# Two expert layers on TensorE: second layer as seven block products (Strassen) instead of eight, in 128x64 tiles

## The chip, the cores and the metric

The kernel runs on one core of a Trainium2 chip. A core has five engines with an instruction queue each: PE (TensorE, matrix products), DVE (VectorE), ACT (ScalarE), POOL (GpSimd) and SP (SyncE, which issues most transfers here). They work on SBUF, a memory of 128 partitions, and on PSUM, eight banks of 128 partitions x 512 f32 in which PE leaves and adds up its products. An instruction waits at the head of its queue for the semaphores that it names, and what stands behind it waits too.

The metric is the device time of one launch, in microseconds (us). All data are f32.

## The reference

The input x is 16 batches of 256 tokens with 128 channels. Four steps each add to x what they compute from its layer norm: attention a (binarized weights, 16 heads of 8), a feed-forward layer of experts, attention b (16 heads, relative positions), and the same expert layer again with the same weights. The expert layer is:

```python
logits = einsum('bld,ed->ble', x, gate_weight)          # 8 experts
kth_val = sort(logits.reshape(-1))[expert_k - 1]         # one threshold over all tokens and experts
gates = logits * (logits >= kth_val)
h = gelu(einsum('bld,ehd->bleh', x, w1) + b1)            # 512 hidden units an expert, tanh form
y = einsum('bleh,edh->blde', h, w2) + b2.T[None, None]
out = einsum('blde,ble->bld', y, gates)
```

All eight experts are computed for every token, and a gate that fails the threshold is a zero factor.

## The kernel before

The kernel is one program for the four steps. An expert layer works on chunks of 512 tokens (`CH`), eight of them, channels on the partitions. One expert on one chunk is called a unit here: 64 units a layer, 128 in all. A unit has a hidden half and an output half, both in `experts`' helpers:

- `h_unit` (L1104, L1106), four times: one matmul of 128 hidden units x 512 tokens, and a gelu on ScalarE that moves the bank to SBUF. Four times 128 hidden units make the expert's 512.
- `y_unit` (L1115): four matmuls that add up, over the 512 hidden units, the 128 output channels x 512 tokens in one bank.
- `gated` (L1231 to L1235): VectorE adds the expert's bias b2 to the bank, multiplies by the gates (`gb`: one gate per token, the same on all partitions) and adds the result to the chunk's accumulator `acc` in SBUF. `gb` comes from `broadcast_gates` (L1209), a transfer that SyncE issues, 256 KB written for 2 KB of gates.
- `residual` (L1258, L1261): when a chunk's eight experts are in `acc`, PE transposes it to token order and VectorE adds it to x.

An f32 matmul is two PE instructions (two passes over the moving data). While PE does the hidden half of unit i, the output half of unit i-1 follows it, so gelu has the time of an output half.

Gates are known only after the threshold, and that comes from a search (`search`, L1157 to L1203: counts on VectorE, small matmuls, 20 rounds) that starts when all logits of the layer are there. So the first `EARLY` = 16 units of each layer are computed without gates: their outputs with bias wait as `raw` tiles (L1134) in SBUF. These early units are interleaved with the end of the attention before (L886, L901, L920 for attention b) and with the search. When the gates exist (L1276, L1282 to L1285), they are multiplied and added (`gated` with bias None), one per late unit, while the other 48 units run.

Between the two layers, attention b begins inside the first: `begin` gives pieces of its preparation (L692 to L832) that are called at four of the last twelve units, and the last chunk's sum of layer one is added to x by `add_late` (L1059, L1064) when attention b is already running.

The order on PE during the search is written by hand; elsewhere a scheduler orders each engine's queue by the program's order, dependences and free buffers.

## Time and profile before

| what | value |
|---|---|
| time, median of 3 runs (lowest, highest) | 1531.12 us (1530.74, 1531.26) |
| span of the profiled execution | 1528.8 us, at full granted clock |
| time outside the span, median less span | 2.3 us |
| PE busy | 1518.9 us, 99% |
| ACT busy | 838.8 us, 55% |
| VectorE busy | 799.5 us, 52% |
| GpSimd busy | 406.0 us, 27% |
| hidden-half matmuls, 1024 instructions | 461.3 us |
| output-half matmuls, 1032 instructions | 462.4 us |
| first early output gated, layer one and two | 400.3 us, 1250.2 us from the span's start |

The time of the profiled execution itself is its span plus what lies around it; the 2.3 us is the difference to the median of the timed runs. Busy times of pipelined matmuls overlap a little, so a line's mean duration (593 ns) is longer than the distance between two starts. In the 40 slices of the page, GpSimd shows 0 or 1 in all slices of the late units and 8 in attention b; VectorE shows 1 to 4 in late units, ScalarE 3 to 5.

A row of a group reads: line, engine, operation, output <- inputs, partitions x elements, number of instructions, then busy microseconds and mean nanoseconds of one, then the engine's idle time just ahead of them and what ended it.

### The profile page before, as it was taken

To read this page: it belongs to the slowest core of one execution; us is meant where nothing else is said; L and a number is where in the kernel's file an instruction comes from. 1 tells how busy PE (TensorE), PEld (TensorE's weight loads), DVE (VectorE), ACT (ScalarE), POOL (GpSimd) and SP (SyncE) were. 2 spreads that over 40 slices of the span, in tenths; PEclk is the share of its full clock that TensorE was granted. 3 is DMA by queue.
4 is the path that set the end of the run, shared out by engine and by line. 5 is a ranking of instruction groups with operands and counts; after the bars stand their busy time and mean duration, and the time that the engine had idled before them with its cause. 6 is when DMAs were issued, how large, how long until landed. Compare 5 with 4: busy or idle time off the path is not lost. (4 is left out here: it accounts for less than half of the span.)

```text
span 1528.8 us, 30857 instructions
## 1 busy us (share of the span) xinstructions
PE 1518.9 (99%) x12284; PEld 856.0 (56%) x12284; DVE 799.5 (52%) x1622; ACT 838.8 (55%) x2092; POOL 406.0 (27%) x521
## 2 busy tenths in 40 slices
PE   9999999999999999999999999999999999999998
PEld 6777777544444444444677777777444444444444
DVE  7878887334334221212799999999244233222212
ACT  4666666645434343443688888888554443434342
POOL 6333321200001000002488898886100000000000
PEclk9999999999999999999999999999999999999999
DMA  4511110000223211121122222221000432111110
GB/s 108 150 30 32 40 30 16 2 7 1 74 74 79 53 37 39 37 46 28 29 54 56 55 51 46 53 56 37 8 1 2 105 87 79 53 44 40 43 41 8
DMA packets 174128, 69.91 MB, mean 46 GB/s; under 512 B 74521, under 2 KB 173601, under 8 KB 173729
## 3 DMA queue, kind: packets, MB, share of 16 engines
q1 hardware_dynamic: 173408, 67.54, 18.9%
q8 instruction: 97, 1.59, 0.4%
q10 hardware_dynamic: 576, 0.41, 0.1%
q14 instruction: 47, 0.38, 0.1%
HBM read 50.88 MB, written 12.58 MB: 42 GB/s over the span
## 5 line engine op out<-in xcount | busy, mean ns | idle before, releaser
L1106 ACT ACTIVATE hT<-ph,head 128x512 f32<-128x512 f32 x512 | 351.2, 687 | 415.3 <-PE ph L1104 412.5
L1115 PE MATMUL py<-hT,w 128*128 128x512 f32 (+1 forms) x1032 | 462.4, 591 | 1.0 <-ACT logits L987 0.5
L1104 PE MATMUL ph<-xn,w 128*128 128x512 f32 x1024 | 461.3, 593 | 1.1 <-ACT hT L1106 1.1
L1104 PEld LDWEIGHTS ph<-xn,w 128*128 128x128 f32 x1024 | 192.7, 190 | 237.0 <-issue 232.4
L1115 PEld LDWEIGHTS py<-hT,w 128*128 128x128 f32 x1032 | 193.7, 190 | 229.7 <-issue 223.4
L1233 DVE SCALAR_TENSOR_TENSOR gy<-py,head,gb 128x512 f32<-128x512 f32 x83 | 62.3, 751 | 427.5 <-PE py L1115 427.5
L901 ACT ACTIVATE b_pr<-b_s,b_nm 128x256 f32<-128x256 f32 x512 | 235.5, 472 | 59.2 <-DVE b_nm L896 59.0
L455 DVE TENSOR_REDUCE a_nm<-a_s 128x2 f32<-128x512 f32 x256 | 158.6, 683 | 50.3 <-PE a_t L478 48.7
L896 DVE TENSOR_REDUCE b_nm<-b_s 128x4 f32<-128x1024 f32 x128 | 152.7, 1193 | 20.1 <-PE b_s L886 19.9
L886 PE MATMUL b_s<-b_kT,b_qd 64*64 64x256 f32 x1024 | 159.8, 382 | 0.0
L911 DVE STREAM_TRANSPOSE b_pT<-b_pr 128x1024 f32<-128x1024 f32 x128 | 157.1, 1228 | 0.0
L886 PE MATMUL b_s<-strip,b_qb 64*64 64x256 f32 x2048 | 156.6, 376 | 0.0
L886 PE MATMUL b_s<-b_kS,b_qd 64*64 64x256 f32 x1024 | 156.5, 382 | 0.0
L484 ACT ACTIVATE a_pT<-a_t 128x512 f32<-128x512 f32 x256 | 132.5, 603 | 29.2 <-PE a_t L478 28.9
L478 PE MATMUL a_t<-a_qa,a_qk 32*128 32x256 f32 x1024 | 133.8, 392 | 0.1
L776 POOL TENSOR_TENSOR b_qd<-b_qsel,head 128x512 f32<-128x512 f32 x64 | 84.1, 1335 | 177.2 <-DMA b_qsel<-b_qT 168.0
L450 PE MATMUL a_s<-a_qk 32*128 32x256 f32 x1024 | 128.2, 389 | 0.3 <-ACT a_qkc L416 0.3
L153 POOL TENSOR_SCALAR ve<-mv 128x2 f32<-128x2 f32 x64 | 14.7, 230 | 418.8 <-DVE mv L150 408.8
L901 ACT ACTIVATION_READ_ACCUMULATOR b_pr<-b_s,b_nm 128x1 f32 x512 | 104.1, 203 | 0.0
L450 PEld LDWEIGHTS a_s<-a_qk 32*128 32x128 f32 x1024 | 91.5, 184 | 22.6 <-issue 14.9
L478 PEld LDWEIGHTS a_t<-a_qa,a_qk 32*128 32x128 f32 x1024 | 99.6, 184 | 4.0 <-PE a_t L478 0.8
L162 POOL TENSOR_SCALAR xn<-x,mv,rstd 128x128 f32<-128x128 f32 x126 | 99.7, 800 | 6.6
(180 smaller groups left out, 1428.4 us busy)
## 6 DMA issues: line engine op xcount, KB each, us to landing
gb<-gd SPq DMA_DIRECT2D x128, 256.0 KB
w<-in_w SPq DMA_DIRECT2D x2, 2048.0 KB
a_qks<-a_qkc SPq DMA_DIRECT2D x15, 256.0 KB
a_qk<-a_qks SPq DMA_DIRECT2D x60, 64.0 KB
x<-in_x SPq DMA_DIRECT2D x16, 128.0 KB
b_qs<-b_qT SPq DMA_DIRECT2D x64, 32.0 KB
b_qsel<-b_qT SPq DMA_DIRECT2D x64, 32.0 KB
b_z<-b_qs SPq DMA_DIRECT2D x16, 128.0 KB
```

The costliest lines, as they stand in the source:

```text
L162: (last or nc.gpsimd).tensor_scalar(xn[:, t, :], xs[b][:, t, :], mv[:, t, 0:1], rstd[:, t : t + 1], ALU.subtract, ALU.mult,)
L450: nc.tensor.matmul(sc[:, t, :], q[b][rows, g, t * P : (t + 1) * P], k[b][rows, g, :], start=True, stop=True,)
L455: nc.vector.tensor_reduce(nms[G % 4][:, :, j, 0:1].rearrange("p t o -> p (t o)"), sc, AX.X, ALU.max, negate=True,)
L478: nc.tensor.matmul(sc[:, t, :], k[b][rows, g, t * P : (t + 1) * P], qaug[G][rows, :], start=True, stop=True,)
L484: nc.scalar.activation(pT, sc, AF.Exp)
L886: nc.tensor.matmul(sc[64 * c : 64 * c + 64, r, u, :], (qb_[rows, at, c] if rel else qd[rows, at, x]).rearrange("p h q -> p (h q)"), strip[ ...
L896: nc.vector.tensor_reduce(nm, sc, AX.X, ALU.max, negate=True)
L901: nc.scalar.activation(pr[:, u, r, :], sc[:, r, u, :], AF.Exp, bias=nm[:, r, u : u + 1], scale=1.0, accum_out=sums[b][:, n : n + 1],)
L911: nc.vector.transpose(pT[:, half % 2, 4 * i : 4 * i + 4].rearrange("p n k h q -> p (n k h q)"), probs.pop(U).rearrange("p u r k -> p (u r ...
L1104: nc.tensor.matmul(ph, w1[:, m * P : (m + 1) * P], xn2[c], start=True, stop=True)
L1106: nc.scalar.activation(hT, ph, AF.Gelu_apprx_tanh, bias=b1[:, m : m + 1], scale=1.0)
L1115: nc.tensor.matmul(py[:, 0:width], w2[:, e * NHC + k, :], hs[k], start=k == 0, stop=k == NHC - 1)
```

## The change

The output half of the late units is written as a Strassen product (in Winograd's form). The 512 hidden units and 512 tokens of `y = w2 h` are cut in blocks: two halves of the output channels (64 each), two halves of the hidden units (256 each), two halves of the tokens (256 each). The ordinary product takes eight block products of 64 channels x 256 hidden units x 256 tokens; the new form takes seven, on sums and differences of the blocks.

- `hidden`: a matmul of 128 hidden units is split into two of 64, on the left and right half of PE's columns (128x64 tiles). The gelu of 128x512 is as before.
- `mix_hidden`, on VectorE: both halves of the hidden values are multiplied by the gates (2 instructions of 128x1024), and four differences of 128x512 are made. On GpSimd: bias times gates, and its sum over a chunk's experts.
- `mix_weights`, on GpSimd, once per expert and layer: four sums and differences of weights, 128x128 each, kept in the buffers of the raw tiles.
- `products`, on PE: 14 matmuls of 256 tokens (7 products, two halves of the contraction each), in pairs on the two column halves. All experts of a chunk add up in two PSUM banks, so there is no accumulation on VectorE.
- `combine`, once per chunk: ScalarE copies the two banks, SyncE issues three transfers that swap partition halves, GpSimd adds the parts and the bias sum.
- `EARLY` is 18. Four early outputs are gated in the first late slot, then one in each slot; the adds of the latter go to GpSimd.
- The last chunk of the second layer keeps the old form (`plain`). The order of the late units is written by hand for all five engines; gates are fetched a slot ahead, behind the transfers of `combine`; residuals come at slots 15, 28 and the end (41 in the second layer); `begin` has three pieces instead of four, at slots 15, 28 and 34; `add_late` comes one round later; the bias copy `bv` is made at the start of attention b.

```diff
@@ -28 @@
-EARLY = 2 * NE
+EARLY = 2 * NE + 2
...
@@ -702 @@
 
         bo = wpool.tile([P, C], F32, tag="bo", name="b_bo_")
 
+        bv = wpool.tile([P, P], F32, tag="bv", name="b_bv_")
+        nc.vector.tensor_copy(bv, b_bv.to_broadcast([P, P]))
+
         def output_bias(pt):
-            bv = wpool.tile([P, P], F32, tag="bv", name="b_bv_")
-            nc.vector.tensor_copy(bv, b_bv.to_broadcast([P, P]))
             nc.tensor.matmul(pt, bv, wb["o"], start=True, stop=True)
             nc.vector.tensor_tensor(bo, b_bo, pt, ALU.add)
 
...
-                if U == 2:
+                if U == NU + 2:
                     add_late()
                 if U < total:
                     scores(U)
@@ -1141 @@
     def experts(last, place, raw, filling, middle, late):
 
         with ExitStack() as st:
-            hpool = st.enter_context(tc.tile_pool(name="f_h", bufs=1))
             pool = st.enter_context(tc.tile_pool(name="f_2", bufs=2))
-            psum = st.enter_context(tc.tile_pool(name="f_ps", bufs=1, space=PSUM))
+            at_first = st.enter_context(ExitStack())
+            hpool = at_first.enter_context(tc.tile_pool(name="f_h", bufs=1))
+            psum = at_first.enter_context(tc.tile_pool(name="f_ps", bufs=1, space=PSUM))
...
             def broadcast_gates(c, e):
-                gb = pool.tile([P, CH], F32, tag="gb", name=f"gb{c}_{e}", bufs=7 if last else 6)
+                gb = pool.tile([P, CH], F32, tag="gb", name=f"gb{c}_{e}", bufs=7 if last else 5)
                 nc.sync.dma_start(
                     gb.rearrange("p (t k) -> p t k", k=P),
                     gd[c * 4 * NE : (c + 1) * 4 * NE, :]
@@ -1214 @@
                 )
                 return gb
 
...
+            accs, fetched = {}, {}
+
+            def gates_of(c, e):
+                if (c, e) not in fetched:
+                    fetched[c, e] = broadcast_gates(c, e)
+                return fetched.pop((c, e))
+
+            def sum_of(c):
+                if c == NCHUNK - 1 and not last:
+                    accs[c] = late
                 else:
+                    accs[c] = pool.tile([P, CH], F32, tag="acc", name=f"acc{c}", bufs=3)
+                return accs[c]
+
+            def gated(c, e, y, bias, adds=nc.vector):
+
+                gb = gates_of(c, e)
+                dst = pool.tile([P, CH], F32, tag="gy", name=f"gy{c}_{e}", bufs=2 if last else 1)
+                first = c not in accs
+                if first:
+                    dst = sum_of(c)
                 if bias is None:
                     nc.vector.tensor_tensor(dst, y, gb, ALU.mult)
                 else:
                     nc.vector.scalar_tensor_tensor(dst, y, bias, gb, ALU.add, ALU.mult)
-                if e:
-                    nc.vector.tensor_tensor(accs[c], accs[c], dst, ALU.add)
+                if not first:
+                    adds.tensor_tensor(accs[c], accs[c], dst, ALU.add)
 
...
             def residual(c, halves=(0, 1)):
-                pr = psum.tile([P, 4, C], F32, tag="m", name=f"f_pr{c}_{halves[0]}", bufs=2)
+                pr = free_bank(f"f_pr{c}_{halves[0]}").rearrange("p (t c) -> p t c", c=C)
...
+            halves = (slice(0, 64), slice(64, 128))
+            mixed, sums, biases = {}, {}, {}
+            firsts = {EARLY // NE: EARLY % NE}
+
+            def mix_weights(e):
+
+                m = pool.tile([P, CH], F32, tag="raw", name=f"mix{e}", bufs=EARLY - 4)
+                m = m.rearrange("p (i k c) -> p i k c", i=4, c=64)
+                ks = [w2[:, e * NHC + 2 * h : e * NHC + 2 * h + 2, :] for h in range(2)]
+                (a11, a21), (a12, a22) = ([k[:, :, z] for z in halves] for k in ks)
+                nc.gpsimd.tensor_tensor(m[:, 0], a21, a22, ALU.add)
+                nc.gpsimd.tensor_tensor(m[:, 1], m[:, 0], a11, ALU.subtract)
+                nc.gpsimd.tensor_tensor(m[:, 2], a11, a21, ALU.subtract)
+                nc.gpsimd.tensor_tensor(m[:, 3], a12, m[:, 1], ALU.subtract)
+                mixed[e] = m
+
+            def hidden(c, e):
+
+                hs = []
+                for k in range(NHC):
+                    if k % 2 == 0:
+                        h = hpool.tile([P, 2, CH], F32, tag="hT", name=f"hT{c}_{e}_{k}", bufs=4)
+                        hs.append(h)
+                    m = e * NHC + k
+                    ph = free_bank(f"ph{c}_{e}_{k}")
+                    for z in halves if c < plain else (slice(0, P),):
+                        nc.tensor.matmul(
+                            ph[z], w1[:, m * P + z.start : m * P + z.stop], xn2[c],
+                            start=True, stop=True,
+                        )
+                    nc.scalar.activation(
+                        h[:, k % 2], ph, AF.Gelu_apprx_tanh, bias=b1[:, m : m + 1], scale=1.0
+                    )
+                return hs
+
+            def mix_hidden(c, e, hs):
+
+                gb = gates_of(c, e)
+                parts = [
+                    hpool.tile([P, 2, T], F32, tag="mx", name=f"mx{c}_{e}_{i}", bufs=6)
+                    for i in range(3)
+                ]
+                t1, t2, t4 = parts
+                (b11, b12), (b21, b22) = ([h[:, :, 0:T], h[:, :, T : 2 * T]] for h in hs)
+                for i, h in enumerate(hs):
+                    nc.vector.tensor_tensor(
+                        h, h, gb.unsqueeze(1).to_broadcast([P, 2, CH]), ALU.mult
+                    )
+                    if not i:
+                        nc.vector.tensor_tensor(t1, b12, b11, ALU.subtract)
+                nc.vector.tensor_tensor(b12, b22, b12, ALU.subtract)
+                nc.vector.tensor_tensor(t2, b22, t1, ALU.subtract)
+                nc.vector.tensor_tensor(t4, b21, t2, ALU.subtract)
+                first = c not in biases
+                if first:
+                    biases[c] = pool.tile([P, CH], F32, tag="bias", name=f"bias{c}")
+                t = biases[c]
+                if not first:
+                    t = pool.tile([P, CH], F32, tag="gy2", name=f"bias{c}_{e}", bufs=2 if last else 1)
+                nc.gpsimd.tensor_scalar(t, gb, b2[:, e : e + 1], None, ALU.mult)
+                if not first:
+                    nc.gpsimd.tensor_tensor(biases[c], biases[c], t, ALU.add)
+                return b11, b21, b22, t1, t2, b12, t4
+
+            def products(c, e, operands):
+
+                first = e == firsts.get(c, 0)
+                if first:
+                    sums[c] = [
+                        psum.tile([P, 2, T], F32, tag=f"s{i}", name=f"s{c}_{i}", bufs=2)
+                        for i in range(2)
+                    ]
+                pa, pb = sums[c]
+                b11, b21, b22, t1, t2, t3, t4 = operands
+                ks = [w2[:, e * NHC + 2 * h : e * NHC + 2 * h + 2, :] for h in range(2)]
+                a11, a12, a22 = ks[0][:, :, halves[0]], ks[1][:, :, halves[0]], ks[1][:, :, halves[1]]
+                m = mixed[e]
+                p1, p2, p6 = (0, pa, 1, a11, b11), (0, pa, 0, a12, b21), (0, pb, 0, m[:, 1], t2)
+                p7, p4, p3 = (1, pa, 1, m[:, 2], t3), (1, pa, 0, a22, t4), (1, pb, 0, m[:, 3], b22)
+                p5 = [(z, pb, 1, m[:, 0], t1) for z in range(2)]
+                order = [
+                    pair for pairs in (
+                        ((p1, 0), (p5[1], 1)), ((p1, 1), (p3, 0)), ((p5[0], 0), (p3, 1)),
+                        ((p2, 0), (p7, 0)), ((p2, 1), (p7, 1)), ((p6, 0), (p4, 0)),
+                        ((p6, 1), (p4, 1)),
+                    ) for pair in pairs
+                ]
+                of = [(p[0], p[1] is pa) for p, _ in order]
+                for i, ((z, acc, col, a, b), k) in enumerate(order):
+                    nc.tensor.matmul(
+                        acc[halves[z], col], a[:, k], b[:, k],
+                        start=first and of[i] not in of[:i],
+                        stop=e == NE - 1 and of[i] not in of[i + 1 :],
+                    )
+
+            def combine(c):
+
+                left, right = halves
+                ab = []
+                for i, s in enumerate(sums.pop(c)):
+                    t = pool.tile([P, 2, T], F32, tag=f"s{i}", name=f"sum{c}_{i}", bufs=1)
+                    nc.scalar.copy(t, s)
+                    ab.append(t)
+                a, b = ab
+                other = pool.tile([P, 3, T], F32, tag="so", name=f"so{c}", bufs=1)
+                nc.sync.dma_start(other[left, 0:2], b[right])
+                nc.sync.dma_start(other[right, 0:2], b[left])
+                nc.sync.dma_start(other[right, 2], a[left, 1])
+                yield
+                early = c in accs
+                acc = (accs[c] if early else sum_of(c)).rearrange("p (n t) -> p n t", t=T)
+                add = lambda z, o, x, y: nc.gpsimd.tensor_tensor(o[z], x[z], y[z], ALU.add)
+                both = slice(0, P)
+                add(left, a[:, 0], a[:, 0], a[:, 1])
+                add(left, a[:, 1], a[:, 1], b[:, 0])
+                add(right, a[:, 1], a[:, 1], other[:, 0])
+                add(right, a[:, 1], a[:, 1], other[:, 2])
+                add(right, a[:, 0], a[:, 0], a[:, 1])
+                add(both, b[:, 1], b[:, 1], other[:, 1])
+                add(both, a[:, 1], a[:, 1], b[:, 1])
+                add(left, a[:, 1], a[:, 1], other[:, 0])
+                if early:
+                    add(both, a, a, acc)
+                add(both, acc, a, biases.pop(c).rearrange("p (n t) -> p n t", t=T))
 
 
...
+            at_first.close()
+            hpool = st.enter_context(tc.tile_pool(name="f_g", bufs=1))
+            psum = st.enter_context(tc.tile_pool(name="f_pg", bufs=1, space=PSUM))
+
+            def free_bank(name):
+                return psum.tile([P, CH], F32, tag="h", name=name, bufs=4)
+
+            place["y"] = (psum, "h", 4)
...
             total = NCHUNK * NE
-            prev, due, ready = None, 0, []
+            plain = NCHUNK - 1 if last else NCHUNK
+            raws = deque([4, 5, 6, 7, 8, 16, 9, 17, *range(10, 16), *range(4)])
+            turn_at = {15: (0, 1, 2), 28: (3, 4)}
+            turn_at[41 if last else total - EARLY] = (5, 6)
+            middle_at = (15, 28, 34)
+            slots, gates_at = [], []
+            for i in range(EARLY, total + 1):
+                mine = [raws.popleft() for _ in range(1 if slots else 4) if raws]
+                slots.append(mine)
+                mine = [divmod(r, NE) for r in mine]
+                c, e = divmod(i, NE)
+                if i < total and c < plain:
+                    mine.append((c, e))
+                if i > EARLY and divmod(i - 1, NE)[0] >= plain:
+                    mine.append(divmod(i - 1, NE))
+                gates_at += [(i - EARLY, ce) for ce in mine]
+            prev, combining = None, None
+
+            def fetch(s):
+                while gates_at and gates_at[0][0] <= s:
+                    ce = gates_at.pop(0)[1]
+                    fetched[ce] = broadcast_gates(*ce)
+
+            fetch(0)
             for i in range(EARLY, total + 1):
                 c, e = divmod(i, NE)
-                hs, now, ready = None, ready, []
+                s = i - EARLY
                 if i < total:
...
                 if i < total:
+                    for done in turn_at.get(s, ()):
+                        residual(done)
+                if middle is not None and s in middle_at:
+                    next(middle(free_bank), None)
+                if i < total:
+                    hs = hidden(c, e)
+                for r in slots[s]:
+                    gated(*divmod(r, NE), raw[r], None, nc.gpsimd if s else nc.vector)
+                if combining:
+                    next(combining, None)
+                    combining = None
+                if prev is not None:
+                    pc, pe, operands = prev
+                    if pc < plain:
+                        products(pc, pe, operands)
+                        if pe == NE - 1:
+                            combining = combine(pc)
+                            next(combining)
+                    else:
+                        hs_ = [h[:, k] for h in operands for k in range(2)]
+                        if i == total:
+                            last_in_halves(pc, pe, hs_)
+                        else:
+                            gated(pc, pe, y_unit(place, pc, pe, hs_), b2[:, pe : pe + 1])
+                if i < total:
+                    if c < plain:
+                        for ahead in (i, i + 1):
+                            if ahead % NE not in mixed:
+                                mix_weights(ahead % NE)
+                        hs = mix_hidden(c, e, hs)
+                    prev = (c, e, hs)
+                fetch(s + 1)
+            if combining:
+                next(combining, None)
+            for done in turn_at.get(total - EARLY, ()):
                 residual(done)
 
```

## The prediction

> **What bounds the kernel now.** I read the page's busy shares first, then its chain, then the groups by line, then the rows of the operations that the change puts elsewhere.
>
> ```profile
> PE 1518.9 (99%) x12284; PEld 856.0 (56%) x12284; DVE 799.5 (52%) x1622; ACT 838.8 (55%) x2092; POOL 406.0 (27%) x521
> PE py L1115 14%; PE ph L1104 13%; PE f_pr L1258 0%; PE pc L1162 0%; DVE x L1261 0%; DVE gy L1247 0%; DVE acc L1250 0%; PE pg L1282 0%; PE pcs L1162 0%; DVEq L1261 0%
> ```
>
> PE is busy 99% and the chain stays on it, on the two expert layers' lines, so time leaves only if PE's own work shrinks and nobody else becomes the slowest. The groups give PE's prices (busy sums; the last two rows are from the groups with shapes kept apart).
>
> ```profile
> L1115 PE MATMUL py<-hT,w 128*128 128x512 f32 (+1 forms) x1032 | 462.4, 591 | 1.0 <-ACT logits L987 0.5
> L1104 PE MATMUL ph<-xn,w 128*128 128x512 f32 x1024 | 461.3, 593 | 1.1 <-ACT hT L1106 1.1
> ```
> ```profile
> L920 PE MATMUL b_m<-b_pT,b_va 128*32 128x128 f32 x2048 | 62.5, 274 | 0.0
> L494 PE MATMUL a_mv<-a_pT,a_va 128*32 128x256 f32 x1024 | 62.1, 382 | 0.0
> ```
>
> A mean of 593 ns includes the pipeline's overlap: eight such instructions (four matmuls, two passes each) start 3.433 us apart in the timeline, 0.429 per pass. So a unit, one expert on 512 tokens, takes 6.87 us: 3.43 for the hidden layer, 3.43 for the output layer.
>
> The pair of tiles that the change uses (128x64) is nowhere in this trace. The nearest are four 128x32 tiles side by side: 1024 instructions of 256 columns in 62.1 us are 256 groups, 0.243 us each with the ends of each batch; inside a batch, groups start 0.216 us apart. Four in 0.216 is the pace of one full tile (0.429 / 2), so side-by-side tiles cost nothing extra there.
>
> The last reading is of VectorE and GpSimd, which the change loads. In f32 from SBUF, VectorE adds 128x512 in 0.69 us and 128x256 in 0.425: 1.04 ns a column and 0.16 fixed, which makes 1.22 for 1024. GpSimd:
>
> ```profile
> L784 POOL TENSOR_TENSOR b_qb<-b_z,head 128x512 f32<-128x512 f32 x64 | 72.9, 1162 | 0.0
> L951 POOL TENSOR_TENSOR x<-x,b_bo__4692 128x256 f32<-128x256 f32 x16 | 11.7, 734 | 0.0
> ```
>
> Its slope is (1162 - 734) / 256 = 1.67 ns a column. Only two moments of the trace have a VectorE instruction with two SBUF inputs beside a GpSimd instruction that reads SBUF, and both stretch (single lines' minimum, median, maximum; then the timeline):
>
> ```profile
> L275 DVE TENSOR_TENSOR sgn_qk<-sgn_qk,a_w x1: 425/425/425, 6.8 to 6.8; 128x256 f32<-128x256 f32 x1
> L275 DVE TENSOR_TENSOR sgn_vp<-sgn_vp,a_w x1: 557/557/557, 11.9 to 11.9; 128x256 f32<-128x256 f32 x1
> ```
> ```profile
> L162 POOL TENSOR_SCALAR xn<-x,mv,rstd x126: 792/802/1042, 10.7 to 1095.1; 128x128 f32<-128x128 f32 x126
> ```
> ```profile
> L1235 DVE TENSOR_TENSOR b_late_sum<-b_late_sum,gy x7: 693/693/737, 697.9 to 735.7; 128x512 f32<-128x512 f32 x7
> ```
> ```profile
> L816 POOL COPY b_va<-b_vz x64: 634/654/811, 697.6 to 1052.3; 32x256 f32<-32x256 f32 x64
> ```
> ```profile
> 697.64 2.91 POOL L816 COPY b_va<-b_vz 32x256 f32<-32x256 f32 x4 [2.13 <-DMA b_vz<-b_vs]
> 697.91 0.74 DVE L1235 TENSOR_TENSOR b_late_sum<-b_late_sum,gy 128x512 f32<-128x512 f32 x1
> ```
>
> At 11.9 us VectorE lost 132 ns to a GpSimd read of 128 columns, and GpSimd lost 240. At 697.9 VectorE began 0.27 us into a copy of some 0.65 and still lost only 44 ns; the next copy lost 157. They take turns, but not for an instruction's whole length. The Trainium skill, SBUF — State Buffer, "Who interferes with whom", says that the pair of ports is locked for the whole instruction and the other side blocks fully; at 697.9 that would have cost VectorE about 0.37 us, and the row says 0.044. By its rule each plain slot would need 5.2 + 2.1 us and the sum of all slots would be about 145 us worse; I don't take it, since the row is of this kernel.
>
> **Part by part.** 84 late units take the new way (46 in the first layer; 38 in the second, whose last chunk keeps the old one).
>
> 1. Hidden layer: each matmul becomes two of 64 output channels. As a concurrent pair, unchanged at 3.43. One after the other it would be +3.4 a unit; the four-tile rows exclude that.
>
> 2. Output layer: 14 matmuls of 256 columns as seven pairs, two passes each: 14 x 0.216 = 3.02 in place of 3.43, a gain of 0.409; 84 of them **-34.4 us**. Upper bound by the 62.1 us row: 14 x 0.243 = 3.40, a gain of 0.03 and 2.6 in all. Nothing speaks for a larger gain. I take 0.216, since the new batches follow each other in one tile shape. Weight loads of 64 columns take 0.132 (four for each 0.216 in the 64x64 scores), so they stay covered.
>
> 3. Changes of tile shape, about 16 (residual transposes, pieces of attention b, weave): starts across a change are 0.33 apart instead of 0.22 in, 0.20 instead of 0.11 out: **+1.6**, bounds 0 and 3.
>
> 4. VectorE: the old multiply-add (0.75 + 0.69 a unit) becomes two products of 1024 and four differences of 512: 2 x 1.22 + 4 x 0.69 = 5.20 a unit; with one early unit's product (0.69) 5.89. PE's slot is now 3.43 + 3.02 = 6.46, so it is covered, with 0.57 left in a slot with an early unit. Its result is needed only after the next unit's hidden layer.
>
> 5. GpSimd: bias product and bias add each unit, the early unit's add in slots 1 to 14, and four differences of 128 columns of weights an expert (slots 0 to 6). An add is 1.16; the product is between 0.6 (its copies) and 2.6 (800 ns for 128 columns with two scalars, scaled), I take 0.9; four differences are about 4 x 0.51. That is 3.2 and 5.3 a slot, below 6.46 alone. What counts is its time on the ports beside VectorE's. VectorE reads for 1.04 x (2 x 1024 + 5 x 512) = 4.79 in an early-unit slot. Taking a GpSimd hold of 132 ns per 128 columns from the 557 ns row, three instructions of 512 hold 1.58, the weights' four 0.53: 6.37 without and 6.90 with weights. Six slots a layer are 0.44 over 6.46: 6 x 0.44 x 2 = **+5**. Bounds: 0 (turns fall into VectorE's 0.16 us gaps), and the rival's price below. Left open is the first slot, where 18 early units keep PE busy until 400.0 + 2 x 6.87 = 413.8 us: gates arrive at 397.8 to 404.6 (six transfers), VectorE's four early products and first differences end near 411, so it is hidden; were those units not there, about 11 us a layer would show.
>
> 6. Chunk's end (`combine`): two ScalarE copies, three transfers, eight or nine GpSimd adds of 256 columns (0.73) and one or two of 512. Two other banks take the next chunk, so PE goes on. Sync issues the next gates behind these transfers, which wait for the copies: gates land about 1.4 + 3.4 = 4.8 us after the last product, differences end 5.2 later, and PE wants them 9.9 after it. Level; **+1.5** over eleven ends, bounds 0 and 11 (1 us each). ScalarE has 4 x 0.69 of 6.46 and is no limit.
>
> 7. End of layer one: the last chunk's copies (1.2), transfers (2) and GpSimd adds (7) stand before GpSimd's first work for attention b, and its first exponential waits on their storage: about 10 us, against eight transposes and woven early units on PE. **+4**, bounds 0 and 6.
>
> 8. Regrouped residuals, three pieces instead of four, the later `add_late`, the hoisted bias copy: the same instructions (0.41 VectorE, eight 0.11 transposes) at other places. Covered by 0.5 us and more of VectorE's slack a plain slot; if that is gone, 0.41 x 16 = 6.5.
>
> Sum: -34.4 + 1.6 + 5 + 1.5 + 4 = -22.3. The profiled span is 1528.8; 1506.5 after, plus the 2.3 between span and median (1531.1): **1509 us**.
>
> **Rivals.**
>
> A. VectorE and GpSimd become the bound (slower). Place: slots 1 to 14 of each layer. GpSimd then holds the ports for its full slope, 0.87 an add (0.52 the product, by a copy's 1035 ns for 1024), 2.26 a slot and 0.87 for weights: 7.05 and 7.92, over by (8 x 0.59 + 6 x 1.46) x 2 = 27; if turns also don't fit VectorE's gaps, 8.15 and 9.02, 58, and 56 plain slots of 6.59 add 7. Middle 46: 1509 - 5 + 46 = **1550**, from 1531 to 1570. It decides from about 1 us over in an average early-unit slot (27 us in 28 slots). For: both stretches exist, and all VectorE operands are now in SBUF. Against: the 44 ns.
>
> B. A pair of 128x64 tiles runs at 0.243: gain 2.6 instead of 34.4, longer slots hide item 5: **1536**. Two full-height moving streams are new; but four are in the L494 row. The skill's TensorEngine Tiling (Array Packing), "Restrictions", says that column tiling switches fast weight load off; no row here shows it hurting.
>
> C. Gates late at the chunk ends and early slots, 1 us at each of 11 ends and one start: +12, **1521**.
>
> D. Nothing gained as PE only waits for something else: then no change, 1531.
>
> **How the numbers follow.** Forecast (1500 to 1520) 0.50, C 0.09, A 0.29, B 0.07, D 0.05. The predicted time is the forecast's; its own range is 1500 to 1520. Range of 8 in 10: A's upper part beyond 1566 and anything below 1499 are left out, some 0.1: **1499 to 1566**. Faster (under 1528; 0.2% is 3 us, what a measurement can tell) 0.59, same 0.05, slower 0.36.
>
> **What the profile after would show.** Starts of products 0.216 apart and a slot of 6.46: item 2. Waits of PE's product line on VectorE in slots 1 to 14, VectorE adds well over 0.69, GpSimd adds over 1.16: A. Pairs 0.243 apart or in turn: B. Waits on gates at chunk ends: C. A wait of ScalarE on GpSimd at the first scores of attention b: item 7. The prediction is wrong if VectorE's sum in an early-unit slot exceeds 6.5 us.

## The result

The changed kernel takes 1623.0 us (median of four runs, 1621.3 to 1624.7), the kernel before 1530.9 in the same comparison: ratio 1.060, 95% interval 1.0587 to 1.0617. It is 92 us slower, where 1509 us was forecast with a range up to 1566.

The page of the changed kernel, busy times and the two groups that grew most:

```profile
PE 1531.9 (95%) x14636; PEld 880.8 (54%) x14636; DVE 1239.0 (77%) x1943; ACT 852.9 (53%) x2118; POOL 955.3 (59%) x867
L1317 DVE TENSOR_TENSOR hT<-hT,gb 128x1024 f32<-128x1024 f32 x168 | 225.3, 1341 | 65.2 <-DMA gb<-gd 33.9
L1331 POOL TENSOR_SCALAR bias<-gb,head 128x512 f32<-128x512 f32 x84 | 221.5, 2637 | 13.5 <-DMA gb<-gd 11.3
```

PE has fallen from 99% to 95%: it waits now. VectorE has gone from 52% to 77%, GpSimd from 27% to 59%. Cutting both spans at the transposes of the gates (first layer, then second) and at the first scores of attention b gives three stretches. The columns are the stretch, its length, busy time (instructions) of PE, PE's weight loads, VectorE, ScalarE and GpSimd, granted clock (the share of TensorE's full clock that the chip allowed), DMA share and GB/s; first the kernel before, then the changed one:

```profile
391.80:736.80 345.00, 344.15 (x840) 154.66 (x838) 89.67 (x149) 136.75 (x202) 20.12 (x25) 1.00 0.21 52
736.80:1183.00 446.20, 444.56 (x6713) 292.52 (x6713) 358.43 (x600) 331.98 (x1224) 282.54 (x329) 1.00 0.19 38
1183.00:1528.80 345.80, 341.44 (x829) 154.10 (x827) 88.73 (x140) 135.02 (x197) 0.00 (x0) 1.00 0.22 55
```
```profile
391.80:785.60 393.80, 352.40 (x2127) 167.47 (x2125) 330.47 (x326) 144.62 (x216) 314.07 (x201) 0.98 0.21 50
785.60:1240.30 454.70, 446.49 (x6714) 293.23 (x6714) 358.79 (x600) 331.92 (x1224) 289.07 (x337) 0.99 0.19 38
1240.30:1619.50 379.20, 344.43 (x1893) 166.06 (x1891) 287.03 (x284) 141.60 (x209) 248.87 (x161) 1.00 0.22 55
```

The expert layers lose 49 and 33 us, attention b 8.5. In the first layer VectorE (the third busy time) goes from 90 to 330 us of some 390, GpSimd (the fifth) from 20 to 314. Who PE waits for: the total in us, how often, and the longest:

```profile
PE s L1361 <- DVE mx L1324: 21.7, 35, 1.0
PE s L1361 <- DVE hT L1317: 20.7, 20, 3.0
PE ph L1298 <- DVE x L1266: 9.5, 4, 3.1
PE b_s L882 <- ACT b_pr L897: 6.6, 3, 6.2
```

And VectorE's instructions in the first layer's late units (busy us, mean ns):

```profile
L1317 DVE TENSOR_TENSOR hT<-hT,gb 128x1024 f32<-128x1024 f32 x92 | 122.8, 1335 | 37.7 <-DMA gb<-gd 21.2 <-ACT hT L1302 16.4
L1321 DVE TENSOR_TENSOR mx<-hT 128x512 f32<-128x512 f32 x46 | 56.2, 1221 | 1.6
L1322 DVE TENSOR_TENSOR hT<-hT,hT 128x512 f32<-128x512 f32 x46 | 52.4, 1139 | 1.6
L1324 DVE TENSOR_TENSOR mx<-hT,mx 128x512 f32<-128x512 f32 x46 | 50.1, 1090 | 4.9 <-DVE mx L1323 0.5
```

The differences take 0.69 us when nothing disturbs them (the shortest of each line, in the same trace), the products 1.21; here three of the four differences average 1.1 to 1.2 us. The mean less the shortest time, times the count, gives 11 + 24 + 21 + 18 us for the four rows, and 6 for the remaining difference: some 80 us lost in this layer. Where the time goes is seen one by one. VectorE, then GpSimd, in 7 us of slots with early outputs (start, duration in us; a slot is the time of one late unit):

```profile
504.60 1.65 DVE L1321 TENSOR_TENSOR mx<-hT 128x512 f32<-128x512 f32 x1
...
507.42 0.98 DVE L1322 TENSOR_TENSOR hT<-hT,hT 128x512 f32<-128x512 f32 x1
...
509.11 1.57 DVE L1324 TENSOR_TENSOR mx<-hT,mx 128x512 f32<-128x512 f32 x1
```
```profile
503.51 2.19 POOL L1240 TENSOR_TENSOR acc<-acc,gy 128x512 f32<-128x512 f32 x1 [1.23 <-DVE gy L1236]
505.69 3.05 POOL L1331 TENSOR_SCALAR bias<-gb,head 128x512 f32<-128x512 f32 x1
508.82 1.31 POOL L1333 TENSOR_TENSOR bias<-bias,bias 128x512 f32<-128x512 f32 x1
```

GpSimd's early addition ends at 505.70, VectorE's difference at 506.25: 0.55 later, about the time that it needs for its 512 columns. GpSimd's bias addition ends at 510.13, VectorE's difference at 510.68: 0.55 again. Of the products and differences (L1317, L1321 to L1324) of both layers' late units, 250 are stretched by over 0.12 us; 137 of 128x512 end some 0.55 us behind a GpSimd instruction and 32 of 128x1024 end some 1.1 behind one (10 end at other distances; in 71 none ended, and they lost some 0.3 each, as the 0.98 above beside the bias product). The constant distance says that in the two groups VectorE does not start to read until GpSimd's instruction has ended. Which began first decides: in the 18 cases where a GpSimd sum or difference began while VectorE's instruction was already running, with no GpSimd instruction beside it when it started, VectorE lost at most 0.02 us.

Theory LOCK: a VectorE instruction with two SBUF inputs waits for the end of certain GpSimd instructions, and this sets the time. Rival LOAD: GpSimd simply has too much to do. Theory GATES: SyncE's queue at the chunk ends sends the gates late.

### The profile page after: what moved, and what is told of

Its sections match the earlier page's. It is cut to its first block, busy times and chain, and to the rows that moved or that the text cites. A ratio compares the mean times of both kernels' runs of the same rounds, so it can differ in the third digit from the quotient of the medians.

```text
span 1619.5 us, 36589 instructions
## 1 busy us (share of the span) xinstructions
PE 1531.9 (95%) x14636; PEld 880.8 (54%) x14636; DVE 1239.0 (77%) x1943; ACT 852.9 (53%) x2118; POOL 955.3 (59%) x867
## 5 line engine op out<-in xcount | busy, mean ns | idle before, releaser
L1302 ACT ACTIVATE hT<-ph,head 128x512 f32<-128x512 f32 x368 | 252.9, 687 | 401.0 <-PE ph L1298 362.0
L1298 PE MATMUL ph<-xn,w 128*64 128x512 f32 (+1 forms) x1408 | 358.3, 598 | 11.5 <-DVE x L1266 9.5
L1317 DVE TENSOR_TENSOR hT<-hT,gb 128x1024 f32<-128x1024 f32 x168 | 225.3, 1341 | 65.2 <-DMA gb<-gd 33.9
L1331 POOL TENSOR_SCALAR bias<-gb,head 128x512 f32<-128x512 f32 x84 | 221.5, 2637 | 13.5 <-DMA gb<-gd 11.3
L1298 PEld LDWEIGHTS ph<-xn,w 128*64 128x64 f32 (+1 forms) x1408 | 124.5, 140 | 185.7 <-issue 159.6
L1361 PE MATMUL s<-mx,mix 128*64 128x256 f32 x672 | 194.8, 391 | 8.8 <-DVE mx L1321 6.2
L1361 PE MATMUL s<-hT,w 128*64 128x256 f32 x672 | 180.8, 386 | 7.1 <-DVE hT L1317 7.0
L1361 PE MATMUL s<-hT,mix 128*64 128x256 f32 x672 | 164.9, 385 | 17.7 <-DVE hT L1317 13.7
L1111 PE MATMUL py<-hT,w 128*128 128x512 f32 (+1 forms) x360 | 160.5, 588 | 1.0 <-ACT hT L1102 0.5
L1100 PE MATMUL ph<-xn,w 128*128 128x512 f32 x288 | 130.7, 594 | 1.1 <-ACT hT L1102 1.1
```

Of the source, the lines that this page charges most:

```text
L1100: nc.tensor.matmul(ph, w1[:, m * P : (m + 1) * P], xn2[c], start=True, stop=True)
L1111: nc.tensor.matmul(py[:, 0:width], w2[:, e * NHC + k, :], hs[k], start=k == 0, stop=k == NHC - 1)
L1298: nc.tensor.matmul(ph[z], w1[:, m * P + z.start : m * P + z.stop], xn2[c], start=True, stop=True,)
L1302: nc.scalar.activation(h[:, k % 2], ph, AF.Gelu_apprx_tanh, bias=b1[:, m : m + 1], scale=1.0)
L1317: nc.vector.tensor_tensor(h, h, gb.unsqueeze(1).to_broadcast([P, 2, CH]), ALU.mult)
L1331: nc.gpsimd.tensor_scalar(t, gb, b2[:, e : e + 1], None, ALU.mult)
```

## The experiments

**The bias addition left out.** In `mix_hidden`:

```diff
-                if not first:
-                    nc.gpsimd.tensor_tensor(biases[c], biases[c], t, ALU.add)
```

> The changed kernel without the GpSimd addition that sums the bias products of a chunk's experts (73 instructions of about 1.4 us, two SBUF inputs); the product stays, so the output lacks most of the late units' bias. Theory LOCK (a VectorE instruction with two SBUF inputs waits for the end of a GpSimd instruction with two SBUF inputs): in the changed kernel 61 of the 144 us that VectorE's instructions lost end right behind this addition; most of it goes, 1570 to 1585 us. Rival LOAD (GpSimd simply has too much to do, and what waits is for its results and the buffers it frees): 106 of its 955 us go, 1605 to 1615.

1581.2 us, 42 less. As LOCK says, beyond what LOAD allows.

**The addition replaced by memsets of its length.**

```diff
-                    nc.gpsimd.tensor_tensor(biases[c], biases[c], t, ALU.add)
+                    nc.gpsimd.memset(t, 0.0)
+                    nc.gpsimd.memset(t, 0.0)
+                    nc.gpsimd.memset(t[:, 0:T], 0.0)
```

> The same addition replaced by three memsets of GpSimd that write 128x512, 128x512 and 128x256 and take the same time in all (about 1.4 us), reading nothing; the output lacks most of the late units' bias. LOCK: as without the addition, 1570 to 1588 us. LOAD: GpSimd is as busy as in the changed kernel, so no change, 1618 to 1628.

1586.2 us: 37 of the 42 go, although GpSimd is busy for 901 us (806 without the memsets, 955 with the addition). What VectorE waits for is what the addition does on SBUF, not that GpSimd is busy.

**The bias product left out.**

```diff
-                if not first:
-                    t = pool.tile([P, CH], F32, tag="gy2", name=f"bias{c}_{e}", bufs=2 if last else 1)
-                nc.gpsimd.tensor_scalar(t, gb, b2[:, e : e + 1], None, ALU.mult)
-                if not first:
-                    nc.gpsimd.tensor_tensor(biases[c], biases[c], t, ALU.add)
+                if first:
+                    nc.gpsimd.tensor_copy(biases[c], gb)
+                else:
+                    nc.gpsimd.tensor_tensor(biases[c], biases[c], gb, ALU.add)
```

> The changed kernel without the GpSimd product of bias and gates (84 instructions, 2.64 us on average, one tensor input and a scalar per partition); the addition stays and adds the gates themselves, so the output's bias is wrong. LOCK: the addition still holds VectorE up and the product had cost it only 1.4 us, so the gain is small for the 221 us that GpSimd sheds: 1590 to 1610 us. LOAD: the largest gain of all, since the longest of its work goes: 1560 or less.

1623.0 us, no change, although GpSimd's busy time falls by 191 us. LOAD falls; LOCK's own range (1590 to 1610) is missed too. VectorE's groups in the first layer show why:

```profile
L1317 DVE TENSOR_TENSOR hT<-hT,gb 128x1024 f32<-128x1024 f32 x92 | 135.9, 1477 | 46.8 <-DMA gb<-gd 28.1 <-ACT hT L1302 18.6
L1321 DVE TENSOR_TENSOR mx<-hT 128x512 f32<-128x512 f32 x46 | 49.2, 1069 | 1.6
```

The addition now starts when the gates arrive and so stands beside the 1.21 us products (1477 on average, 1335 with the bias product in front); the differences gain about what the products and the early products lose.

**Chunk-end transfers issued by ScalarE.** The three lines of `combine` that start with `nc.sync.dma_start(other[...` become `nc.scalar.dma_start(...`.

> The changed kernel with the three transfers of each chunk's end issued by ScalarE instead of SyncE, so that gates behind them are no longer held up. Theory GATES (SyncE's queue at the chunk ends is a main cause): VectorE waited 34 us for gates in front of its products and 25 us in front of the early ones; 1590 to 1605. LOCK: most of these waits come from gate buffers that GpSimd frees late, 1612 to 1623.

1610.5 us, 12.5 less: neither GATES (1590 to 1605) nor nothing. VectorE's wait for gates in front of its products falls from 33.9 us in 7 times to one of 3.9. The queue is a real cost, at about a seventh of the 92 us.

**What locks.** In the kernel before, where PE is the bound and VectorE has time, idle work on GpSimd beside `gated`'s addition, another kind in each chunk (the first layer has five gate buffers instead of six, to make room for `out`):

```diff
...
+                g, out = nc.gpsimd, pool.tile([P, CH], F32, tag="beside", name="beside", bufs=1)
+                g.tensor_copy(out[:, 0:1], gy[:, 0:1])
+                u, v, q = w1[:, 0:CH], w1[:, CH : 2 * CH], slice(0, 32)
+                for _ in range({2: 6, 3: 5, 4: 13, 5: 13, 6: 6, 7: 9}[c]):
+                    if c == 2:
+                        g.tensor_tensor(out, u, v, ALU.add)
+                    elif c == 3:
+                        g.tensor_scalar(out, u, b2[:, 0:1], None, ALU.mult)
+                    elif c == 4:
+                        g.tensor_copy(out, u)
+                    elif c == 5:
+                        g.memset(out, 0.0)
+                    elif c == 6:
+                        g.tensor_tensor(out[q], u[q], v[q], ALU.add)
+                    else:
+                        g.tensor_scalar(out, u, 2.0, None, ALU.mult)
```

> The kernel before, with idle work on GpSimd beside VectorE's additions of the first layer's late units (128x512, two SBUF inputs, 0.69 us alone), another kind in each chunk, back to back for some 7 us a unit: chunk 2 a sum of two 128x512 inputs; chunk 3 a 128x512 input times a scalar per partition; chunk 4 a copy of 128x512; chunk 5 a memset; chunk 6 a sum of two 32x512 inputs; chunk 7 a 128x512 input times a constant. The results are used by nobody. LOCK BY TWO INPUTS (my reading of the changed kernel): the additions go up to 1.2 to 1.9 us in chunks 2 and 6 and end some 0.55 us after a GpSimd instruction; at most 0.3 us over in chunks 3, 4 and 7, where GpSimd's instruction is stretched instead; 0.69 in chunk 5. LOCK BY ANY READ (whole instruction, whatever GpSimd reads): as in chunk 2 in chunks 3, 4 and 7 too. VectorE's product with a PSUM input keeps its 0.75 us everywhere. Time as before within 5 us, as PE is the bound.

VectorE's groups in the stretches of chunks 2, 3, 4, 5 and 6, and GpSimd's in the same ones:

```profile
L1235 DVE TENSOR_TENSOR acc<-acc,gy 128x512 f32<-128x512 f32 x16 | 23.5, 1496 | 0.0
L1235 DVE TENSOR_TENSOR acc<-acc,gy 128x512 f32<-128x512 f32 x12 | 7.9, 688 | 0.1
L1235 DVE TENSOR_TENSOR acc<-acc,gy 128x512 f32<-128x512 f32 x7 | 7.4, 1061 | 0.2
L1235 DVE TENSOR_TENSOR acc<-acc,gy 128x512 f32<-128x512 f32 x7 | 4.8, 692 | 0.2
L1235 DVE TENSOR_TENSOR acc<-acc,gy 128x512 f32<-128x512 f32 x5 | 5.4, 1073 | 0.2
```
```profile
L1246 POOL TENSOR_TENSOR beside<-w 128x512 f32<-128x512 f32 x42 | 60.5, 1440 | 3.3
L1248 POOL TENSOR_SCALAR beside<-w,head 128x512 f32<-128x512 f32 x35 | 57.2, 1633 | 3.2
L1250 POOL COPY beside<-w 128x512 f32<-128x512 f32 x91 | 58.1, 639 | 5.6
L1252 POOL MEMSET beside<- 128x512 f32 x91 | 47.7, 524 | 5.3
L1254 POOL TENSOR_TENSOR beside<-w 32x512 f32<-32x512 f32 x42 | 55.1, 1313 | 3.2
```

Both readings that stood against each other were wrong. A sum of two inputs holds VectorE up (1496 on average, most at 1.75), on 32 partitions as well (1073); but a copy, with one input, does it too (1061), and a product with a scalar, which also reads SBUF, does not (688, and 692 beside the product with a constant in chunk 7, 1.49 us each). A memset does not. All stretched additions end 0.54 to 0.56 us behind a GpSimd instruction. VectorE's instruction with a PSUM input keeps 0.75 everywhere. So it is the kind of GpSimd instruction that decides, and for a sum or a copy of these shapes it holds for the instruction's whole length, if GpSimd began first. Where VectorE began first, it is GpSimd that waits (the sum alone takes 1.26):

```profile
475.00 0.69 DVE L1231 TENSOR_TENSOR gy<-raw,gb 128x512 f32<-128x512 f32 x1 [8.13 <-POOL beside L1242]
475.05 1.77 POOL L1246 TENSOR_TENSOR beside<-w 128x512 f32<-128x512 f32 x1
```

The time of this run (1640 us, expected as before) was missed for another reason: GpSimd's stretched work is longer than a unit, and VectorE waited 223 us for a buffer that the first copy of each series had not yet read. The durations don't depend on that wait.

**The bias on PE.** Gates of four token tiles x eight experts stand on 32 partitions; one matmul of 32 rows per chunk gives the bias of 512 tokens, added to x. GpSimd's product and sum go, the early outputs are kept without bias; the transfers are on ScalarE.

```diff
+            for c in range(NCHUNK - 1 if last else NCHUNK):
+                rows = slice(32 * (c % 4), 32 * (c % 4) + 32)
+                pb = psum.tile([P, CH], F32, tag="m", name=f"f_pb{c}", bufs=2)
+                nc.tensor.matmul(pb, gTs[c // 4][rows], b2s[rows], start=True, stop=True)
...
-                nc.gpsimd.tensor_scalar(t, gb, b2[:, e : e + 1], None, ALU.mult)
-                if not first:
-                    nc.gpsimd.tensor_tensor(biases[c], biases[c], t, ALU.add)
...
```

> The changed kernel with the bias done by PE: right after the gates are known one matmul of 32 rows per chunk (gates of four token tiles x eight experts, times a block matrix of b2) and two VectorE additions to x; early outputs are kept without bias, GpSimd has neither bias product nor sum. The chunk-end transfers are issued by ScalarE as in the run with that change alone. LOCK: 42 us as without the addition, 12 as with the transfers moved, less about 9 of PE's time for the matmuls: 1570 to 1582 us. If something else than the lock set the time in the runs so far, no more than the transfers' 12: 1610.

1584.9 us, 3 above the range: the first late unit starts 13.7 us later in the first layer (428.1 against 414.4) and, counted from the gates, 13 later in the second, where 9 had been put for both layers together.

**Early additions on VectorE.**

```diff
-                    gated(*divmod(r, NE), raw[r], None, nc.gpsimd if s else nc.vector)
+                    gated(*divmod(r, NE), raw[r], None, nc.vector)
```

> The version with the bias on PE, with one more edit: the early outputs' additions in slots 1 to 14 go from GpSimd to VectorE (24 of 0.69 us in all). GpSimd keeps the chunk ends and the weight differences. In the trace without this edit VectorE's instructions lost 23 us behind GpSimd's additions of early outputs and 23 behind those of the chunk ends. LOCK: 23 lost against 17 of own work, nearly even for VectorE, but the waits of residuals on GpSimd's sums go as well (3.6): 1575 to 1585, and the larger part of the step to the version with all additions moved (1552.7) belongs to the chunk ends and the residuals' place. If the early outputs' additions are the larger part: 1565 or less.

1579.0 us, 6 less, as expected. (This run was made last; the next expectation means the version with the bias on PE, 1584.9 us, when it says the version before.)

**All other additions on VectorE.** `combine` adds on VectorE, with transfers that put p1, p3, p5 and p6 where full-height additions can use them, so that six are enough; residuals one at a time.

```diff
-                add = lambda z, o, x, y: nc.gpsimd.tensor_tensor(o[z], x[z], y[z], ALU.add)
+                add = lambda z, o, x, y: nc.vector.tensor_tensor(o[z], x[z], y[z], ALU.add)
...
+                add(left, a[:, 0], a[:, 0], a[:, 1])
+                add(both, a[:, 1], a[:, 1], other[:, 2])
+                add(both, a[:, 1], a[:, 1], other[:, 0])
+                add(right, a[:, 0], a[:, 0], a[:, 1])
+                add(both, b[:, 1], b[:, 1], other[:, 1])
+                add(both, a[:, 1], a[:, 1], b[:, 1])
...
-            turn_at = {15: (0, 1, 2), 28: (3, 4)}
-            turn_at[41 if last else total - EARLY] = (5, 6)
+            turn_at = {11: (1,), 13: (2,), 16: (0,), 18: (3,), 26: (4,), 34: (5,), 42: (6,)}
```

> The version before this one, and GpSimd's other additions moved to VectorE too: the early outputs' sums (0.69 us in 14 slots a layer) and the chunk ends' (six of 256 columns, transfers arranged so that six are enough); each chunk's residual stands alone, behind the hidden layer. GpSimd keeps the four weight differences of an expert. LOCK: VectorE instructions keep their own times, slots with an early output need 5.2 + 1.4 = 6.6, the others reach PE's 6.46: 1515 to 1528 us. If VectorE's own work were the limit: VectorE has about 40 us more to do than in the version before, 1580 or more.

1552.7 us. Giving VectorE more work took 26 us off the version just above, against the rival; but the range (1515 to 1528) is missed by 25. The trace shows two places: the late units start 12 us later than in the changed kernel in both layers, counted from the gates, and there is one wait for gates of 8.8 us behind the transfers of attention b's preparation.

**Both mended.** Bias matmuls in pairs on two row groups with four steps of early units between pairs, and gates two slots ahead, in seven buffers:

```diff
-                fetch(s + 1)
+                fetch(s + 2)
...
+                for _ in range(4):
+                    next(filling, None)
```

> The version with GpSimd's additions moved to VectorE, mended in two places that its trace shows: the bias matmuls stand in pairs on two row groups of PE, four early matmul steps apart, so that PE need not wait for VectorE's additions (the first late unit came 12 us later than in the changed kernel, in each layer); and gates are fetched two slots ahead into seven buffers, so that they are not late behind attention b's transfers (one wait of 8.8 us). If these are the causes of what is left: 12 + 12 less 2 x 5 for the matmuls themselves, and 5 to 9 for the gates: 1528 to 1537. If VectorE at 90% busy is a limit by itself, 1545 or more.

1533.8 us, ratio 1.0021 (1.0012 to 1.0030) to the kernel before. VectorE is busy 88% of 500 to 705 us there, and PE 99%: in that stretch its load is no limit by itself.

**The seven products undone in that version.** The hidden layer in full tiles, four full matmuls a unit into one bank, no differences:

```diff
+                for k, h in enumerate(operands):
+                    nc.tensor.matmul(
+                        sums[c], w2[:, e * NHC + k, :], h,
+                        start=first and not k, stop=e == NE - 1 and k == NHC - 1,
+                    )
...
```

> The same version with the seven block products undone: four 128x128 matmuls of 512 tokens a unit on gated inputs, the experts of a chunk still summed in PSUM, no differences of hidden values or weights, one copy at a chunk's end. If the product form is worth what the distance of the starts says (0.409 us a unit, 84 units) and nothing of it is lost, this is 34 us above the version with seven products, less some 5 of its chunk ends and shape changes: 25 to 35 above. If VectorE's differences cost in that version what PE gains, within 8 of it.

1543.1 us, 9.3 above the version with seven products, where 25 to 35 were expected, or up to 8 if VectorE's differences cost what PE gains. With seven products the median slot does go from 6.87 to 6.46 us. But the stretches from the gates to the next scores or the end are only 7.6 and 8.0 us shorter, since its longer slots, most of them at chunk ends and early outputs, exceed the median by some 36 us in all and those of the other form by some 15; and attention b's stretch is 6.1 longer (452.4 against 446.3 us from the first scores to the second layer's gates).

**Early outputs off the slots of the first chunk end; then also the last chunk of layer one in the old form.**

```diff
-                mine = [raws.popleft() for _ in range(1 if slots else 4) if raws]
+                mine = [raws.popleft() for _ in range(0 if len(slots) in (7, 8) else 1 if slots else 6) if raws]
```

> The mended version with six early outputs instead of four in the first late slot, then one a slot, and none in slots 7 and 8, where VectorE also adds up the first finished chunk: in its trace PE waits 3.3 us there and 1.1 two slots on, in each layer. If these waits are lost time of PE: 8 us less, 1523 to 1528. If another wait of the same length follows, 1531 to 1535.

1527.0 us, ratio 0.9977 (0.9967 to 0.9986).

```diff
-            plain = NCHUNK - 1 if last else NCHUNK
+            plain = NCHUNK - 1
```

> The same, and the last chunk of the first layer in the old form too (eight units of 6.87 instead of 6.46 us, no chunk end in front of attention b). PE waited 3.5 us there for ScalarE's first exponential and 1.4 for its copy. Cost 8 x 0.409 = 3.3, gain up to 6: 1520 to 1528, 0 to 3 below the run without it. If the 3.5 us come from elsewhere in attention b's start, 3 above it.

1525.9 us, ratio 0.9968 (0.9956 to 0.9981): 0.3% faster than the kernel before, and its median slot, 6.46 us, is the forecast's. It is still 17 us above the forecast time. VectorE's differences in the first layer, and PE's products between 500 and 640 us:

```profile
L1325 DVE TENSOR_TENSOR mx<-hT 128x512 f32<-128x512 f32 x38 | 27.7, 728 | 1.3
L1328 DVE TENSOR_TENSOR mx<-hT,mx 128x512 f32<-128x512 f32 x38 | 28.1, 739 | 3.8
```
```profile
L1356 PE MATMUL s<-mx,mix 128*64 128x256 f32 x168 | 46.7, 380 | 0.0
```

The differences that averaged 1.1 to 1.2 us are at 0.73, and the products that use them show no wait in that stretch (0.0 behind the bar).

## Why the prediction was wrong

The step that failed is item 5's, in two terms. The first is "Taking a GpSimd hold of 132 ns per 128 columns from the 557 ns row", which makes 0.53 us for an instruction of 512 columns. The changed kernel's bias addition stretched the 65 VectorE instructions of 512 columns that ended 0.55 us behind it by 60 us, 0.93 each: the hold is the whole instruction for a sum, and what VectorE loses depends on how much of it is left when VectorE arrives. The 44 ns that spoke against this were the end of a hold, met late. VectorE and GpSimd in the kernel before, then the same kind of copy in the changed kernel:

```profile
697.91 0.74 DVE L1235 TENSOR_TENSOR b_late_sum<-b_late_sum,gy 128x512 f32<-128x512 f32 x1
697.64 0.64 POOL L816 COPY b_va<-b_vz 32x256 f32<-32x256 f32 x1 [2.13 <-DMA b_vz<-b_vs]
```
```profile
708.05 0.95 DVE L1323 TENSOR_TENSOR mx<-hT,mx 128x512 f32<-128x512 f32 x1
707.82 0.82 POOL L817 COPY b_va<-b_vz 32x256 f32<-32x256 f32 x1
```

Both VectorE instructions end 0.37 us behind the copy, and the two other 128x512 differences that such copies stretch in the changed kernel end 0.37 and 0.38 behind. That is a constant distance again, only 0.18 shorter than the 0.55 of the larger instructions. By it, as an estimate, the copy at 697.64 held VectorE until 698.10, 0.19 us after VectorE's addition had begun; with 0.55 from there instead of 0.69 in all, that costs some 0.05. The other moment, at 11.9 us, was a product with scalars, a kind that does not hold VectorE as a sum does, and it was not true that all such moments stretch: the two-input instruction just before it, at 11.44 us, ran beside the same GpSimd products in 0.41 us. No row of that trace has a GpSimd sum of 128x512 beside a VectorE instruction with two SBUF inputs.

The second term is VectorE's own time. Item 5 set the holds beside the 4.79 us in which VectorE reads, as if the fixed 0.16 us of its seven instructions, 1.1 in all, could take the holds in. They did not. Three slots of the changed kernel, one with an early unit and two without (columns as above):

```profile
511.21:519.05 7.84, 6.81 (x46) 3.25 (x44) 7.67 (x8) 2.75 (x4) 6.53 (x3) 1.00 0.25 69
568.58:575.16 6.58, 6.58 (x46) 3.18 (x44) 6.41 (x7) 2.75 (x4) 6.40 (x3) 1.00 0.27 64
575.16:582.41 7.25, 6.81 (x48) 3.18 (x44) 7.08 (x8) 2.75 (x4) 6.88 (x5) 1.00 0.03 6
```

VectorE is busy from end to end. Its undisturbed times are item 4's, 5.89 and 5.20, and the stretching of 2.1, 1.5 and 2.1 us comes on top; the terms of item 5 make 6.37 and 5.3. So the prediction's own sign of being wrong came: VectorE's sum in an early-unit slot exceeds 6.5 us. Its item 4 time of 5.89 with its own hold of 1.58 would have made 7.47 there, over PE's 6.46; over all early-unit slots that is some 35 us instead of the 5 that it took, an estimate from its own terms. Rival A's upper price for this slot, 8.15, has both terms right in kind.

The page that the prediction set aside, the Trainium skill, SBUF — State Buffer, "Who interferes with whom", came nearer: its whole-instruction rule made the sum 145 us worse, and the chip gave 114 above the forecast. That the totals are so close is in part luck, since the 114 contain the transfers, the residuals and the clock below, which the 145 do not. The rule is right here for sums and copies; beside a product with a scalar or a constant, which also read SBUF, no run showed VectorE blocked for the instruction (beside the changed kernel's bias product it lost at most 0.42 us).

- Items 1 and 2 held as prices. Products start 0.215 us apart in pairs, and two dozen slots of the changed kernel are 6.46 us; rival B is out. As a gain the 34 us did not arrive even without the lock: undoing the seven products in the mended version costs 9.3.
- Item 4's own times held (1.21 and 0.69 undisturbed). "So it is covered, with 0.57 left" did not: 80 us of stretching in 46 units is 1.7 us a unit.
- Item 5's product of bias and gates, taken at 0.9 of bounds 0.6 and 2.6, is 1.56 alone and 2.64 on average, because VectorE's work stretches it. Leaving it out gained nothing, though the addition moved with it in that run.
- Item 6, taken at 1.5 us with a bound of 11, is 12.5 by the run with the transfers moved. What was missed besides: gate buffers come free only when GpSimd, held up by VectorE, has read them; SyncE waited 111 us in 24 times for that behind the bias product, which cost time only where VectorE then had to wait too.
- Item 7, taken at 4 with a bound of 6, is 6.6 us of PE's wait for ScalarE's first exponentials.
- Item 8, costed at nothing: PE waited 9.5 us in 4 times for the additions of residuals that come three or two in a row behind VectorE's late queue.
- Rival A had the right engines and the right sign, but its place, slots 1 to 14, was too narrow and its top, 1570, too low: the largest single part that a run took out is the bias addition of every unit, 42 us.

A cost that no item had: behind long waits PE runs at about half speed for some 3 us. From 536 to 542 us it waited for an early sum and then 3.1 us for residuals; that stretch and the next (columns as above, the clock is the third number from the end):

```profile
536.00:542.00 6.00, 1.77 (x16) 1.61 (x16) 5.86 (x8) 0.51 (x2) 4.10 (x2) 0.94 0.36 84
542.00:545.00 3.00, 3.00 (x8) 1.01 (x10) 1.94 (x9) 0.69 (x1) 0.95 (x3) 0.55 1.03 285
```

At a clock of 0.55 the hidden layer's matmul pairs start 0.85 to 0.88 us apart instead of 0.43. The Trainium skill, TensorE: Matmul & The Clock Gate, Part 1, describes such a halving after an idle window of about 3.4 us; here PE had been busy 1.8 of 6 us, and its longest idle stretch was 3.1. There are six such stretches in the changed kernel, 27.3 us at a clock of 0.50 in which PE is busy for 21.5; half of that, some 11 us, is an estimate of what they cost. The kernel before has none inside its span (granted clock 1.000).

How the parts of the 114 us add up is settled only roughly: the runs overlap (42 for the bias addition, 12.5 for the transfers, 6 for the early additions, 26 for chunk ends and residuals together), and the residuals' share of the last was not tried alone. The last 17 us, from the best version to the forecast, are open: its slots with early outputs and its chunk ends are longer than 6.46, but no run took these apart.

## What to carry to other kernels

Before an engine with slack is given work, look not at its busy share but at whom its instructions block: a GpSimd sum or copy in SBUF stops a VectorE instruction with two SBUF inputs that comes behind it until it has ended, so moving an addition from VectorE to GpSimd can cost VectorE more than doing it. To find such a lock, subtract the end of the other engine's instruction from the end of the stretched one: a constant difference, equal to the work that is left, is its signature. Look at that difference before a small loss is read as a small price: the loss also depends on when the second instruction came. Add such waits to the whole time of the engine that waits, not to its reading time. And a single undisturbed moment of one instruction form is no price for another form: take the end of the range that the rule gives until a row of the same form shows less.

## What the runs showed that was not expected

- GpSimd's product of a 128x512 tile with a scalar per partition takes 1.56 us alone, with a constant 1.49, a copy of it 0.61, a sum 1.26; sum and copy hold VectorE's two-input instructions for their length, both products do not. The product with a scalar per partition is itself stretched (median 2.93 in the changed kernel); the one with a constant stayed at 1.49 beside single VectorE additions.
- A sum on 32 partitions takes as long as on 128 (1.25) and holds VectorE as well.
- The granted clock of 0.55 for 3 us behind one of PE's longest waits.
- Leaving out GpSimd's bias product, 191 us less of GpSimd's busy time, was worth nothing (1623.0 with and without).
